# Attention fused with its graph prologue: ScalarE's and VectorE's instructions in the order of writing

## The chip, the cores and the metric

The kernel runs on one core of a Trainium2 chip. The metric is the device time of one execution in microseconds (us), as the median of several; it is compared between the kernel before and the kernel after the change.

## The reference

Inputs are x of 16 x 1024 x 256 (batch, nodes, channels) and adj of 1024 x 1024, all float32. Two layers are computed, each `x = layernorm(x + layer(x))`. The change concerns the first:

```python
fea = transpose(x, (0, 2, 1))                       # b, c, n
c_adj = mean(fea, axis=1)
diff = c_adj[:, None, :] - c_adj[:, :, None]
A = abs(abs(sigmoid(diff) - 0.5) - 0.5) * 2.0
Wg = adj * (A + transpose(A, (0, 2, 1))) * 0.5
g = relu(einsum('bcn,bnm->bcm', fea, Wg) * para)
q = g, transposed and split in 4 heads of 64
k, v = (x @ kv_w), split in 4 heads of 64
out = softmax(q @ k.T * scale) @ v
x = layernorm(x + out)
```

The second layer aggregates x with a normalised adj, and applies a linear layer, a batch normalisation, a relu, another linear layer and another batch normalisation. The changed lines do not touch it.

## The kernel before, in words

The work of the first layer goes batch element by batch element; what belongs to one of the 16 is called a block here. A block has two parts. The *prologue* (L642 to L748) makes q, k and v. The *attention* (L751 on) uses them. The prologue of block b + 1 is spread over the attention of block b, so that TensorE (PE) always has matmuls to do.

The prologue of a block has three lists. `first` holds four transposes of x through PE (`transpose_x`, L666, each into a PSUM tile of 512 columns that VectorE copies out, L674). The first of them also calls `begin` (L652): VectorE sums x over the channels (`csum`, L657) and makes `ccol` and `ncol`, SyncE's queue writes `ncol` to DRAM (L662) and reads it back spread over all partitions as `crow` (L664). `steps` holds 24 pieces for PE: four `values` (L720) and four `keys` (L708) in turn, and then 16 `graph_mm` (L689), of which four make one quarter of q: PE sums eight products of x with the weights `wg`, VectorE scales the sum (L703) and ScalarE applies relu (L706). `side` holds the pieces that make the eight weight tiles `wg` of 128 x 1024: ScalarE's abs (`weights_abs`, L679), ScalarE's tanh (L684) and, in the same piece as the tanh, VectorE's product with adj (L685).

The attention of a block has 2 pairs of heads times 2 halves of the queries times 8 key chunks, 32 units. A unit is: `scores` (L760), where PE writes 128 x 1024 scores into PSUM and ScalarE makes the exp (L773) into a tile `p`; and `outputs` (L776), where PE multiplies `p` with v (L789) and VectorE adds `p` to the running row sums `acc` (L796 and L798). After the eighth chunk ScalarE and VectorE take the sums of the outputs out of PSUM as `oT` (L802, L803). Two bursts later `normalise` (L805) sums `acc` over the partitions on PE, ScalarE and VectorE add the halves (`drow`, L818, L819), and SyncE's queue turns the row into a column by way of DRAM (L821, L824). Later still `residual` (L829) takes the reciprocal, transposes `oT` on PE (`poT`, L835), multiplies (`o`, L839), and GpSimd (POOL) adds the product to x (L844). After the last unit of a block the same function runs `layernorm` (L580 to L592) on the whole tile: eight statistics with their aggregates on VectorE, two small operations on POOL (L577, L579), eight scalings on VectorE (L590), and a store of x1 from POOL's queue (L847).

Two units make a *burst*; a block has 16, numbered u = 0 to 15. In each burst PE does the scores of this burst and then the outputs of the burst before, and then what the plan places there. `FULL` names the bursts that take four `steps`: 0, 4, 6, 8, 10, 12. Bursts 0 and 4 hold values and keys, the other four a quarter of q each. `residual` goes into bursts 8, 12, 0 and 4, `normalise` into 5, 9, 13 and 1. The two transposes of burst 10 and the two of burst 12 belong to the x of block b + 2, whose load is issued in burst 5. Before the first block a starting stretch makes the prologue of block 0 and the transposes of block 1.

What sets the order of the instructions: inside `tc.manual_schedule` (L862) PE issues in the order of writing. The other engines' order is made by the Tile scheduler, which may move an instruction ahead of others on its engine. The tiles come from pools: the scores have two PSUM tiles (`ps_s`), everything else in the prologue and in `normalise` and `residual` shares two PSUM tiles (`ps_t`, function `tile_t`), the outputs have two; `p` has four tiles, `wg` eight, `crow` one, x three.

Of the kernel before, what the change touches and what calls it, by code (L numbers as in the profile page):

```python
# [515 lines left out]
def fast_path(  # L516
# [19 lines left out]
    nc = tc.nc  # L536
# [3 lines left out]
    NCH = N // P  # L540
# [15 lines left out]
    def tile_t(name):  # L556
        return ps_t.tile([P, HALF], F32, tag="t", name=name)
# [4 lines left out]
    x1_d = [dram.tile([P, NCH, C], F32, tag=f"x1_{b}", name=f"x1_{b}") for b in range(B)]  # L562
# [11 lines left out]
    def rsqrt(dst, src, eps):  # L574
        n = dst.shape[1]
        if eps:
            nc.gpsimd.tensor_scalar(dst, src, eps, None, ALU.add)  # L577
            src = dst
        nc.gpsimd.tensor_tensor(dst, src, mhalf[:, :n], ALU.pow)  # L579

    def layernorm(t, name):
        st = small.tile([P, NCH, 6], F32, tag="ln_st", name=f"st_{name}")
        mv = small.tile([P, NCH, 2], F32, tag="ln_mv", name=f"mv_{name}")
        rstd = small.tile([P, NCH], F32, tag="ln_rs", name=f"rs_{name}")
        for n in range(NCH):
            nc.vector.bn_stats(st[:, n, :], t[:, n, :])
            nc.vector.bn_aggr(mv[:, n, :], st[:, n, :])
        rsqrt(rstd, mv[:, :, 1], EPS)
        for n in range(NCH):
            nc.vector.tensor_scalar(  # L590
                t[:, n, :], t[:, n, :], mv[:, n, 0:1], rstd[:, n : n + 1], ALU.subtract, ALU.mult
            )  # L592
# [20 lines left out]
    with (  # L613
# [15 lines left out]
        st = {}  # L629

        def load_x(b):
            t = xp.tile([P, NCH, C], F32, tag="x", name=f"x_{b}")
            nc.sync.dma_start(t, x[b].rearrange("(n p) c -> p n c", p=P))
            st[b] = {"x": t}
# [7 lines left out]
        def prologue(b):  # L642


            s = st[b]
            xt = s["x"]
            first, steps, side = [], [], []
# [34 lines left out]
            def weights_tanh(n):  # L682
                w = s["wg", n]
                nc.scalar.activation(w, w, AF.Tanh, scale=0.5)  # L684
                nc.vector.scalar_tensor_tensor(  # L685
                    w, w, 1.0, adj_s[:, n, :], op0=ALU.subtract, op1=ALU.mult
                )
# [57 lines left out]
            for n in range(NCH):  # L745
                side.append((weights_abs, (n,)))
                side.append((weights_tanh, (n,)))
            return first, steps, side  # L748


        PAIRS = H // 2  # L751
# [8 lines left out]
        def scores(i):  # L760
            b, pr, qh, m = units[i]
            qT, kT = st[b]["qT"], st[b]["kT"]
            ps = tile_s(f"ps_{i}")
            for kh in range(2):
                for hd in range(2):
                    r = slice(hd * D, (hd + 1) * D)
                    ks = slice(m * P + kh * D, m * P + (kh + 1) * D)
                    nc.tensor.matmul(  # L768
                        ps[kh * D : (kh + 1) * D, hd * HALF : (hd + 1) * HALF], kT[r, pr, ks],
                        qT[r, pr, qh * HALF : (qh + 1) * HALF], start=True, stop=True,  # L770
                    )
            p = pp.tile([P, N], F32, tag="p", name=f"p_{i}")
            nc.scalar.activation(p, ps, AF.Exp)  # L773
            A[i] = p

        def outputs(i):  # L776
            b, pr, qh, m = units[i]
            s, p = st[b], A.pop(i)
            if m == 0:
                G[b, pr, qh] = {  # L780
                    "po": [tile_o(f"po_{i}_{kh}") for kh in range(2)],
                    "acc": accp.tile([P, N], F32, tag="acc", name=f"acc_{i}"),
                }
            g = G[b, pr, qh]
            for hd in range(2):
                h = 2 * pr + hd
                for kh in range(2):
                    r = slice(kh * D, (kh + 1) * D)
                    nc.tensor.matmul(  # L789
                        g["po"][kh][hd * D : (hd + 1) * D, :], s["v"][r, m, h * D : (h + 1) * D],  # L790
                        p[r, hd * HALF : (hd + 1) * HALF], start=(m == 0), stop=(m == NCH - 1),
                    )
            if m == 0:
                g["p0"] = p
            elif m == 1:
                nc.vector.tensor_add(g["acc"], g.pop("p0"), p)  # L796
            else:
                nc.vector.tensor_add(g["acc"], g["acc"], p)  # L798
            if m == NCH - 1:
                k = (b * PAIRS + pr) * 2 + qh  # L800
                g["oT"] = op.tile([P, HALF], F32, tag="oT", name=f"oT_{k}")
                nc.scalar.copy(g["oT"], g["po"][0])  # L802
                nc.vector.tensor_add(g["oT"], g["po"][1], g["oT"])  # L803
# [25 lines left out]
        def residual(b, pr, qh):  # L829
            g, s = G.pop((b, pr, qh)), st[b]  # L830
            k = (b * PAIRS + pr) * 2 + qh
            nc.vector.reciprocal(r_all[:, k], g["col"])
            pt = tile_t(f"poT_{k}")
            for j in range(4):
                nc.tensor.transpose(  # L835
                    pt[:, j * P : (j + 1) * P], g["oT"][:, j * P : (j + 1) * P], ident
                )
            o = rdp.tile([P, 4, 2, D], F32, tag="o", name=f"o_{k}")
            nc.vector.tensor_mul(  # L839
                o, pt.rearrange("p (n h d) -> p n h d", h=2, d=D),  # L840
                r_all[:, k].unsqueeze(3).to_broadcast([P, 4, 2, D]),
            )
            xs = s["x"][:, 4 * qh : 4 * qh + 4, pr * P : (pr + 1) * P]
            nc.gpsimd.tensor_tensor(xs, xs, o.rearrange("p n h d -> p n (h d)"), ALU.add)  # L844
            if pr == PAIRS - 1 and qh == 1:
                layernorm(s["x"], f"l0_{b}")
                nc.gpsimd.dma_start(x1_d[b], s["x"])  # L847
                del st[b]

        def run(fs, k):  # L850
            for f, a in fs[:k]:
                f(*a)
            del fs[:k]
# [1 line left out]

        FULL = {0: 4, 4: 4, 6: 4, 8: 4, 10: 4, 12: 4}
        BURST = 2
        bursts = [range(i, i + BURST) for i in range(0, len(units), BURST)]  # L860
        PERB = PER // BURST
        with tc.manual_schedule(engines={mybir.EngineType.PE}):  # L862
            load_x(1)
            first, steps, side = prologue(0)
            run(first, 4)
            while steps:
                run(side, 4)
                run(steps, 2)
            next_first, next_steps, next_side = prologue(1)
            run(next_first, 4)  # L870
            run(next_side, 6)
            full, quarter = {}, {}

            def back(j):

                for i in bursts[j]:
                    outputs(i)
                b, pr, qh, m = units[bursts[j][-1]]
                if m == NCH - 1:
                    quarter.setdefault(j + 2, []).append((normalise, (b, pr, qh)))  # L880
                    k = j + 5
                    while k % PERB not in FULL:
                        k += 1
                    full.setdefault(k, []).append((residual, (b, pr, qh)))

            for j in range(len(bursts)):
                b, u = j // PERB, j % PERB
                for i in bursts[j]:
                    scores(i)
                run(quarter.get(j, []), 9)  # L890
                if u == 0:
                    steps, side = next_steps, next_side
                    next_first, next_steps, next_side = [], [], []
                if u == 5 and b + 2 < B:
                    load_x(b + 2)
                    next_first, next_steps, next_side = prologue(b + 2)
                if j:
                    back(j - 1)
                if u in FULL:
                    run(full.get(j, []), 9)  # L900
                    run(steps, FULL[u])
                    if u >= 10:
                        run(next_first, 2)
                if u > 12:
                    run(next_side, 2)
                else:
                    run(side, 1 if u in FULL else 2)
            j = len(bursts)
            back(j - 1)
            for k in range(j, j + 8):  # L910
                run(quarter.get(k, []), 9)
                run(full.get(k, []), 9)

        top = l0c.tile([P, 2], F32, name="top")
        nc.vector.tensor_reduce(top[:, 0:1], r_all, AX.XYZ, ALU.max)
# [275 lines left out]
```

## Time and profile before

| what | value |
|---|---|
| median of three runs | 2997.59 us (2993.03 to 2997.8) |
| profiled execution, its own time | 2992.18 us |
| profiled execution, its span | 2990.3 us |
| granted PE clock, mean | 0.947 |
| first scores (L768) start | 81.24 us |
| attention's last exp starts | 1862.38 us |
| one block (1004.36 to 1119.36) | 115.0 us |
| PE busy in that block | about 108.8 us of 115 |

The profile is one execution, recorded by the hardware. Times are counted from the span's start. A line of a timeline gives the start, the length, the engine, the source line, the operation with output and inputs, how many were merged, and in brackets how long the engine stood idle before it and what ended that wait. One burst of scores or outputs is 16 matmul instructions on PE. A busy time of PE is modelled at its end, so distances from start to start are used where it matters.

The attention stretch lasts from about 81 to 1866 us, the second layer fills the rest.

### The profile page before, as it was taken

How to read it: one execution, taken by the hardware profiler on the slowest of the kernel's cores; microseconds unless marked ns; L12 is line 12 of the kernel's file. 1: busy time of each engine (PE TensorE's matmuls, PEld its weight loads, DVE VectorE, ACT ScalarE, POOL GpSimd, SP SyncE). 2: the span in 40 equal slices, each digit the busy share in tenths (PEclk: the TensorE clock that was granted, in tenths of full speed). 3: DMA queues.
4: the chain of work that ended last, by engine and by line, in shares of the span. 5: the costliest groups of instructions: out<-in, count | busy, mean ns of one | idle time of the engine just before them, and what ended most of it. 6: DMA issues, size and time to landing. Idle time of an engine off the chain costs nothing. (4 is left out here: it accounts for less than half of the span.)

```text
span 2990.3 us, 32734 instructions
## 1 busy us (share of the span) xinstructions
PE 2736.4 (92%) x13522; PEld 1202.2 (40%) x13522; DVE 1418.0 (47%) x2130; ACT 1138.6 (38%) x1313; POOL 185.7 (6%) x196
## 2 busy tenths in 40 slices
PE   6999999999999999999999999799999999999842
PEld 3433334333333333334333333544444444344432
DVE  3565555655655665655655647511111212233464
ACT  3555354553553553553544535001101111233383
POOL 0000000000000000000000001000000000000032
PEclk9999999999999999999999999699999999999955
DMA  4001101101101001011011010022121220244265
GB/s 134 8 1 36 36 1 36 30 8 36 29 8 37 29 8 37 10 28 36 1 36 36 1 49 24 29 84 112 57 84 71 84 84 32 123 159 150 84 211 198
DMA packets 122062, 169.00 MB, mean 57 GB/s; under 512 B 86704, under 2 KB 103600, under 8 KB 111664
## 3 DMA queue, kind: packets, MB, share of 16 engines
q1 hardware_dynamic: 112720, 99.70, 10.9%
q0 software_dynamic: 9184, 67.12, 5.7%
q8 instruction: 108, 1.77, 0.3%
q14 instruction: 50, 0.41, 0.0%
HBM read 99.36 MB, written 67.44 MB: 56 GB/s over the span
## 5 line engine op out<-in xcount | busy, mean ns | idle before, releaser
L773 ACT ACTIVATE p<-ps 128x1024 f32<-128x1024 f32 x512 | 498.7, 1018 | 275.5 <-PE ps L768 263.6
L768 PE MATMUL ps<-qT,kT 64*64 64x512 f32 x4096 | 519.1, 619 | 69.6 <-ACT p L773 69.6
L798 DVE TENSOR_TENSOR acc<-acc,p 128x1024 f32<-128x1024 f32 x384 | 470.7, 1226 | 187.9 <-ACT p L773 174.8
L789 PE MATMUL po<-p,v 64*64 64x512 f32 x4096 | 500.4, 599 | 0.0
L697 PE MATMUL pg<-wg,x 128*128 128x512 f32 x1024 | 454.4, 597 | 4.3 <-ACT kT L718 4.3
L1003 PE MATMUL pagg<-ahT,x1l 128*128 128x512 f32 x1024 | 444.0, 593 | 0.0
L1022 ACT ACTIVATE hw<-ph,col_b 128x1024 f32<-128x1024 f32 x64 | 71.2, 1113 | 652.7 <-PE ph L1018 652.7
L768 PEld LDWEIGHTS ps<-qT,kT 64*64 64x64 f32 x4096 | 150.9, 137 | 368.1 <-issue 234.2
L1003 PEld LDWEIGHTS pagg<-ahT,x1l 128*128 128x128 f32 x1024 | 194.3, 190 | 241.1 <-issue 241.1
L697 PEld LDWEIGHTS pg<-wg,x 128*128 128x128 f32 x1024 | 190.2, 190 | 246.3 <-issue 216.6
L789 PEld LDWEIGHTS po<-p,v 64*64 64x64 f32 x4096 | 166.3, 137 | 292.8 <-issue 289.6
L1082 PE MATMUL po<-hl,w2T 128*128 128x512 f32 x512 | 222.8, 598 | 6.9 <-ACT hl L1073 6.9
L1018 PE MATMUL ph<-agg,w1T 128*128 128x512 f32 x512 | 222.2, 592 | 0.0
L1007 DVE COPY agg<-pagg 128x1024 f32<-128x1024 f32 x32 | 39.1, 1223 | 377.9 <-PE pagg L1003 377.9
L706 ACT ACTIVATE qT<-qT 128x512 f32<-128x512 f32 x64 | 40.1, 626 | 407.3 <-DVE qT L703 407.3
L685 DVE SCALAR_TENSOR_TENSOR wg<-wg,adj_s 128x1024 f32<-128x1024 f32 x128 | 153.3, 1220 | 77.0 <-ACT wg L684 77.0
L844 POOL TENSOR_TENSOR x<-x,o 128x512 f32<-128x512 f32 x64 | 81.1, 1267 | 1670.3 <-DVE o L839 1670.3
L1024 DVE BATCH_NORM_STATS2 bn_st<-hw 128x6 f32<-128x512 f32 x128 | 82.3, 685 | 152.4 <-ACT hw L1022 152.4
L727 PE MATMUL pv<-kvw_s,xT 128*128 128x256 f32 x512 | 128.0, 394 | 26.8 <-DVE v L731 16.1
L1082 PEld LDWEIGHTS po<-hl,w2T 128*128 128x128 f32 x512 | 98.3, 192 | 131.4 <-issue 121.9
L679 ACT ACTIVATE wg<-crow,ccol 128x1024 f32<-128x1024 f32 x128 | 140.8, 1137 | 17.2 <-PE pg L697 11.9
L1018 PEld LDWEIGHTS ph<-agg,w1T 128*128 128x128 f32 x512 | 97.3, 190 | 122.5 <-issue 122.5
(87 smaller groups left out, 1962.8 us busy)
## 6 DMA issues: line engine op xcount, KB each, us to landing
h<-hw POOLq DMA_DIRECT2D x16, 2048.0 KB, 6.6
hl<-h SPq DMA_DIRECT2D x16, 2048.0 KB
x<-in_x_dram SPq DMA_DIRECT2D x16, 1024.0 KB
x<-x POOLq DMA_DIRECT2D x16, 1024.0 KB, 4.3
x1l<-x SPq DMA_DIRECT2D x16, 1024.0 KB
xf<-x SPq DMA_DIRECT2D x16, 1024.0 KB
out_dram<-xf POOLq DMA_DIRECT2D x16, 1024.0 KB, 5.4
crow<-c SPq DMA_DIRECT2D x16, 512.0 KB
```

The source lines that it names most:

```text
L679: nc.scalar.activation(w, s["crow"], AF.Abs, bias=s["ccol"][:, n : n + 1])
L685: nc.vector.scalar_tensor_tensor(w, w, 1.0, adj_s[:, n, :], op0=ALU.subtract, op1=ALU.mult)
L697: nc.tensor.matmul(ps, xt[:, n, c * P : (c + 1) * P], s["wg", n][:, hs], start=(n == 0), stop=(n == NCH - 1),)
L727: nc.tensor.matmul(pt[:, j * C : (j + 1) * C], s["xT"][:, c, n * P : (n + 1) * P], kvw_s[:, c, C : 2 * C], start=(c == 0), stop=(c == CC - 1),
L768: nc.tensor.matmul(ps[kh * D : (kh + 1) * D, hd * HALF : (hd + 1) * HALF], kT[r, pr, ks], qT[r, pr, qh * HALF : (qh + 1) * HALF], start=Tr ...
L773: nc.scalar.activation(p, ps, AF.Exp)
L789: nc.tensor.matmul(g["po"][kh][hd * D : (hd + 1) * D, :], s["v"][r, m, h * D : (h + 1) * D], p[r, hd * HALF : (hd + 1) * HALF], start=(m = ...
L798: nc.vector.tensor_add(g["acc"], g["acc"], p)
L1003: nc.tensor.matmul(ps[:, hs], xt[:, m, c * P : (c + 1) * P], ahT[:, m, hs], start=(m == 0), stop=(m == NCH - 1),)
L1018: nc.tensor.matmul(ps[:, hs], w1T[:, c, k * P : (k + 1) * P], t[:, c, hs], start=(c == 0), stop=(c == CC - 1),)
L1024: nc.vector.bn_stats(bn1_st[:, k, 2 * b + half, :], ht[:, k, half * HALF : (half + 1) * HALF])
L1082: nc.tensor.matmul(ps[:, hs], w2T[:, k, c * P : (c + 1) * P], ht[:, k, hs], start=(k == 0), stop=(k == HC - 1),)
```

## The change

ScalarE and VectorE are added to the engines that issue in the order of writing. To suit that, the pieces of the prologue are placed anew: the product with adj becomes a piece of its own (`weights_adj`), one weight behind the tanh; a table `SIDE` says how many side pieces follow each burst, and bursts 0 and 4 take two side pieces after each of their four steps; one of the two transposes in bursts 10 and 12 moves ahead of the graph matmuls; the layernorm of a block becomes a function of its own (`finish_x1`), which is run in the burst after the last residual (burst 5), ahead of the x load and prologue of block b + 2. At the start, six side pieces instead of four go with two steps, and four side pieces of block 1 instead of six stand ahead of block 0. The set of computing instructions is the same, and each is of the same size.

```diff
@@ prologue
             def weights_tanh(n):
                 w = s["wg", n]
                 nc.scalar.activation(w, w, AF.Tanh, scale=0.5)
+
+            def weights_adj(n):
+                w = s["wg", n]
                 nc.vector.scalar_tensor_tensor(
                     w, w, 1.0, adj_s[:, n, :], op0=ALU.subtract, op1=ALU.mult
                 )
...
             for n in range(NCH):
                 side.append((weights_abs, (n,)))
                 side.append((weights_tanh, (n,)))
+                if n:
+                    side.append((weights_adj, (n - 1,)))
+            side.append((weights_adj, (NCH - 1,)))
@@ residual
-            if pr == PAIRS - 1 and qh == 1:
-                layernorm(s["x"], f"l0_{b}")
-                nc.gpsimd.dma_start(x1_d[b], s["x"])
-                del st[b]
+
+        def finish_x1(b):
+            xt = st.pop(b)["x"]
+            layernorm(xt, f"l0_{b}")
+            nc.gpsimd.dma_start(x1_d[b], xt)
@@ the plan
-        FULL = {0: 4, 4: 4, 6: 4, 8: 4, 10: 4, 12: 4}
...
-        with tc.manual_schedule(engines={mybir.EngineType.PE}):
+        FULL = (0, 4, 6, 8, 10, 12)
+        SIDE = {13: 1, 14: 1, 15: 1, 1: 1, 2: 1, 3: 1, 5: 4}
+        with tc.manual_schedule(engines={mybir.EngineType.PE, mybir.EngineType.Activation, mybir.EngineType.DVE}):
             load_x(1)
             first, steps, side = prologue(0)
             run(first, 4)
             while steps:
-                run(side, 4)
+                run(side, 6)
                 run(steps, 2)
             next_first, next_steps, next_side = prologue(1)
             run(next_first, 4)
-            run(next_side, 6)
-            full, quarter = {}, {}
+            run(next_side, 4)
+            full, quarter, late = {}, {}, {}
...
                     full.setdefault(k, []).append((residual, (b, pr, qh)))
+                    if pr == PAIRS - 1 and qh == 1:
+                        late.setdefault(k + 1, []).append((finish_x1, (b,)))
...
                     next_first, next_steps, next_side = [], [], []
+                if j:
+                    back(j - 1)
+                run(late.get(j, []), 9)
                 if u == 5 and b + 2 < B:
                     load_x(b + 2)
                     next_first, next_steps, next_side = prologue(b + 2)
-                if j:
-                    back(j - 1)
                 if u in FULL:
                     run(full.get(j, []), 9)
-                    run(steps, FULL[u])
                     if u >= 10:
-                        run(next_first, 2)
-                if u > 12:
-                    run(next_side, 2)
+                        run(next_first, 1)
+                    for _ in range(4):
+                        run(steps, 1)
+                        if u <= 4:
+                            run(side, 2)
+                    if u >= 10:
+                        run(next_first, 1)
+                elif u > 12:
+                    run(next_side, SIDE[u])
                 else:
-                    run(side, 1 if u in FULL else 2)
+                    run(side, SIDE.get(u, 0))
```

More of the change, by code (lines that the diff above doesn't have):

```diff
@@ L912, in fast_path @@
                 run(full.get(k, []), 9)
+                run(late.get(k, []), 9)
         top = l0c.tile([P, 2], F32, name="top")
```

## The prediction

> **What bounds the kernel now.** I read the busy shares and slices first, then PE's waits between 100 and 1850 us, then one block (one batch element's attention, 16 bursts) as a timeline, engine by engine, then the start. TensorE is 92% busy, VectorE 47%, ScalarE 38%: only time in which PE stands still, or runs slowly, can be won.
>
> ```profile
> PE 2736.4 (92%) x13522; PEld 1202.2 (40%) x13522; DVE 1418.0 (47%) x2130; ACT 1138.6 (38%) x1313; POOL 185.7 (6%) x196
> ```
>
> PE's waits in the attention stretch (engine, line, awaited: us, times, longest): the scores wait for the exp that frees their PSUM tile. Values wait for a copy, transposes for the q eviction.
>
> ```profile
> PE ps L768 <- ACT p L773: 69.6, 20, 4.5
> PE pv L727 <- DVE v L731: 12.7, 14, 0.9
> PE pxT L671 <- DVE qT L703: 9.7, 28, 0.3
> ```
>
> One such wait on PE's timeline, at the end of a block: 4.45 us idle, then a burst of 3.69 us and one of 2.59 instead of 1.9.
>
> ```profile
> 1103.57 1.92 PE L789 MATMUL po<-p,v 64*64 64x512 f32 x16
> 1109.94 3.69 PE L768 MATMUL ps<-qT,kT 64*64 64x512 f32 x16 [4.45 <-ACT p L773]
> 1113.41 2.59 PE L789 MATMUL po<-p,v 64*64 64x512 f32 x16
> 1115.83 1.89 PE L768 MATMUL ps<-qT,kT 64*64 64x512 f32 x16
> ```
>
> ScalarE at that moment: weight pieces stand ahead of the two exps, whose scores were written by 1103.7.
>
> ```profile
> 1103.95 1.06 ACT L684 ACTIVATE wg<-wg 128x1024 f32<-128x1024 f32 x1
> 1104.91 2.18 ACT L679 ACTIVATE wg<-crow,ccol 128x1024 f32<-128x1024 f32 x2
> 1106.99 1.99 ACT L684 ACTIVATE wg<-wg 128x1024 f32<-128x1024 f32 x2
> 1108.88 1.91 ACT L773 ACTIVATE p<-ps 128x1024 f32<-128x1024 f32 x2
> ```
>
> VectorE's layernorm holds a round trip through POOL; the start has ScalarE waiting for crow, then the first exp at 83.41:
>
> ```profile
> 1034.15 2.67 DVE L590 TENSOR_SCALAR x<-x,mv_l,rs_l 128x256 f32<-128x256 f32 x8 [2.12 <-POOL rs_l L579]
> 36.46 2.19 ACT L679 ACTIVATE wg<-crow,ccol 128x1024 f32<-128x1024 f32 x2 [5.29 <-DMA crow<-c]
> 83.41 1.00 ACT L773 ACTIVATE p<-ps 128x1024 f32<-128x1024 f32 x1
> ```
>
> **What the Trainium skill says.** "TensorE: Matmul & The Clock Gate", Part 1: an idle window of about 3.4 us halves PE's clock, and busy time restores it. The trace agrees: all 14 waits of 4.45 us are followed by a burst of 3.00 to 3.69 us; the one of 2.07 us by 2.46, one of 1.42 by 2.00. The same page, Architectural detail: ScalarE and VectorE queues are strict FIFO; the exps above show it. "ScalarE: Activation LUTs", Table sets: exp, tanh and abs share one set, so interleaving them loads no tables; the trace has one load (1.28 us) in all. "VectorE: DVE Perf Modes", The DRAIN you can't avoid: a semaphore on the engine's own last result costs nothing beyond the drain. The trace differs a little: two accumulations that depend on each other stand 1.31 us apart, two independent weight products 1.14.
>
> **The change, part by part.** Both orders were read from the built programs. Durations are of the profiled execution.
>
> *Removed.* (1) Weight pieces now stand singly between bursts (abs in 13, tanh in 14, abs in 15), the rest under the wide bursts 0 and 4. A plain burst has 3.43 us of PE against 1.94 for two exps, so a piece of 1.04 to 1.14 fits. The 14 waits go: each is 4.65 (idle between planned and real start) plus 1.75 and 0.70 of slow clock, 7.1 us: 99.4. (2) Layernorm leaves bursts 0 and 4: 15 value waits of 0.91: 13.7. (3) One transpose moves ahead of the graph matmuls: 28 x 0.35: 9.8. (4) The mean of the next x moves from VectorE's place right behind the load to burst 10: four waits of exps, 5.0. Together 128.
>
> *Added at burst 6, blocks 1 to 14.* VectorE's order in burst 5 is: denominator row, one accumulation, whole layernorm, weight products 6 and 7. From the start of burst 5: ScalarE has the last k copy to 0.7 (0.58), abs to 1.7, tanh to 2.8 (it waits for abs), two exps to 4.65, row copy to 5.15. VectorE, behind that copy: row add 0.68 and accumulation 1.22, to 7.0; eight statistics, each 0.39 plus an aggregate of 0.17 that waits for it, 4.0 to 4.5, to 11.3; POOL 2.12, to 13.4; eight scalings 2.67, to 16.05; product 6 at 17.2, 7 at 18.4. PE: burst 5 is 1.77 + 0.86 + 1.72 = 4.35, burst 6's scores and outputs 3.54, six of eight graph products 5.23: it needs weight 6 at 13.1. Gap 4.1 us, and with it the slow clock of a 4.45 gap, 2.45: 6.55 x 14 = 91.7. Queued behind on VectorE are the accumulations that free p for the exps of burst 7; at slow clock PE comes there later than they do (0), at full clock 0.5 us late.
>
> *Added at burst 12.* The new transpose stands between poT and the graph, and both PSUM tiles are then taken. The graph waits for o, which now stands behind the oT add, behind ScalarE's oT copy: copy ends 4.25 us after the burst's start, add 5.0, reciprocal 5.1, o 5.85; PE was ready at 4.6: 1.3 x 14 = 18.2. In bursts 0 and 4 k waits likewise, 0.13 x 29 = 3.8.
>
> *Added at the start.* VectorE and ScalarE can't run ahead any more. Table load behind crow's wait: abs starts at 37.8 not 36.46. Values copies and k copies stand among the weight pieces; eight pairs of 2.15 and two k copies of 0.6 end at 56.5, the last k copy at 57.1, graph from there instead of 49.0: ends 86.0 instead of 78.3. Only then does VectorE take block 1's x mean (2.29 + 0.25, it ran at 34.51 and before), then the write of c (SP's wait for it: median 8.1, 8.5 in the block read) and crow (4.06 from issue to use at the start): abs of block 1 at 101.9. Two abs/tanh pairs of 2.15 stand ahead of the first exp: 106.2 instead of 83.41. PE stands still for a k tile meanwhile; burst 2 starts at 116.5 instead of 95.2: 21. Bounds: c 8.1 to 10.9, crow 2 to 4.1, PE cold or not: 18 to 26.
>
> *Last block, 3.4.* In burst 5 layernorm has no wide burst over it: the row copy comes earlier (exps from 1.1 to 3.05, copy 3.65), row add and accumulation end at 5.5, statistics at 9.8, POOL 11.95, scalings 14.6, and the exps of burst 7 wait for accumulation 5 at 15.8, where they could start at 8.9; PE loses 6.2, 8.6 with its clock, where the block loses 5.2 now. *After attention, 6.5.* Four of the eight row sums of adj ran beside PE's column sums; in the new order all eight stand behind the weight copies that need PE: 4 x 1.34, and the check of the denominators, which PE's column sums stand behind, comes 1 later. SP's and POOL's order of DMAs stays: the x load waits for the x1 store, which ends some 18 us ahead of its use at burst 10, and that is free.
>
> Sum: -128 + 91.7 + 18.2 + 3.8 + 21 + 3.4 + 6.5 = +16.6 us. Made against the profiled execution (span 2990.3, time 2992.2) it gives 3008.8; the median shown is 2997.6, 5.4 above it, so I forecast 3014.
>
> What is unseen is a layernorm as one block on VectorE (4.0 to 4.5 for its statistics; POOL 1.65 to 2.12), and a gap of 3 to 4 us: its clock loss lies between 0.5 (the 2.07 gap) and 2.45. Burst 6 thus costs 3.5 to 7.2, 49 to 101 in all; I take 6.55, since every gap near it paid in full.
>
> **Rivals.** *A, faster:* the chain in burst 5 ends earlier, or PE's idle time stays under what trips the clock. Decides at a gap of about 3 us: then 3 + 1.2 = 4.2 x 14 = 59, and the sum is -16: 2981; at 2 us, -41: 2957. For it: statistics that overlap as they do now, the next starting before an aggregate ends. Against: every link has its row. *B, all stalls go:* layernorm hides, PE is fed throughout: -75, 2922. Against: PE's queue reaches weight 6 at 13.1, and layernorm alone is 9. *C, slower still:* late accumulations hold the exps of bursts 6 to 8 too, or the statistics take over 5 us: 1 to 1.8 more a block, or the start 5 more: 3035. *D, nothing changes:* needs an unchanged order; 14 blocks have another.
>
> **How the numbers follow.** A measurement can tell about 0.2% (6 us) from no change. Forecast 0.55, its own range 2997 to 3030; A 0.26, B 0.04, C 0.14, D 0.01. Faster: A mostly and B: 0.28. Same: the lower edge of the forecast and A's upper: 0.12. Slower 0.60. The range cuts B, a little of A and of C: 2964 to 3042.
>
> **What would show it.** The exp's 4.45 waits gone; a wait of graph matmuls (L700 in the changed file) for the weight products (L688 there) of about 4 us, 14 times, with a slow burst behind; waits of graph for o (L845 there), 1.3 us, 14 times; the first exp near 106; the attention's end later by some 10 us; adj's scaling later still by 6. Wrong if the L700 wait is under 3 us or the clock holds, or the first exp comes before 100.

## The result, and the profile after

| | before | after |
|---|---|---|
| median, us | 2995.59 (2993.03 to 2997.8) | 2995.57 (2991.16 to 2996.58) |
| profiled execution, its own time | 2992.18 | 2996.41 |
| its span, and granted PE clock | 2990.3, 0.947 | 2994.5, 0.944 |

The ratio of after to before is 0.9997 (95% interval 0.998 to 1.0015): no difference that can be measured. The forecast was 3014 us, slower.

PE is 91% busy, VectorE 48%, ScalarE 38%, nearly as before. PE's waits between 100 and 1850 us in the profile after, all of them (engine, line, awaited; us in total, times, longest):

```profile
PE pg L700 <- DVE wg L688: 54.7, 14, 3.9
PE pg L700 <- DVE o L845: 18.5, 14, 1.3
PE pk L717 <- DVE v L734: 11.4, 1, 11.4
PE ps L774 <- ACT p L779: 5.3, 1, 5.3
```

So the 20 waits for exps (one is left, in the last block), the value waits and the transpose waits are gone. In their place stand the graph's waits for a weight product and for `o`, and one wait at the start. Bursts 14 and 15, which held a stall of 4.45, now take 3.43 us each in every block.

Here is a burst 6 on PE's timeline; its burst 5 began at 925.92.

```profile
933.80 5.42 PE L700 MATMUL pg<-wg,x 128*128 128x512 f32 x12
943.13 3.21 PE L700 MATMUL pg<-wg,x 128*128 128x512 f32 x4 [3.91 <-DVE wg L688]
946.27 2.56 PE L774 MATMUL ps<-qT,kT 64*64 64x512 f32 x16
948.66 1.89 PE L795 MATMUL po<-p,v 64*64 64x512 f32 x16
```

Twelve instructions run, then PE waits 3.91 us; the next four take 3.21 instead of 1.88, and the scores 2.56 instead of 1.95. VectorE holds it up, with accumulation, layernorm and products one after the other (most of the statistics are left out at the dots):

```profile
931.69 1.22 DVE L802 TENSOR_TENSOR acc<-p,p 128x1024 f32<-128x1024 f32 x1
932.82 0.42 DVE L586 BATCH_NORM_STATS2 st_l<-x 128x6 f32<-128x256 f32 x1
...
939.27 2.67 DVE L590 TENSOR_SCALAR x<-x,mv_l,rs_l 128x256 f32<-128x256 f32 x8 [2.12 <-POOL rs_l L579]
941.86 2.35 DVE L688 SCALAR_TENSOR_TENSOR wg<-wg,adj_s 128x1024 f32<-128x1024 f32 x2
```

The start: ScalarE waits 17.36 us for the crow of block 1, and the exps of burst 0 come at 110.23 instead of 83.41, behind two pairs of abs and tanh.

```profile
105.96 1.15 ACT L679 ACTIVATE wg<-crow,ccol 128x1024 f32<-128x1024 f32 x1 [17.36 <-DMA crow<-c]
110.23 1.92 ACT L779 ACTIVATE p<-ps 128x1024 f32<-128x1024 f32 x2
```

Burst 12, then adj's first transposes behind the attention (their wait was 8.29):

```profile
986.59 3.70 PE L700 MATMUL pg<-wg,x 128*128 128x512 f32 x8 [1.32 <-DVE o L845]
1924.54 1.05 PE L1004 MATMUL pah<-ident,adj_s 128*128 128x128 f32 x2 [14.10 <-DVE adj_s L999]
```

Distances between the starts of successive bursts of scores on PE give a ledger of the whole difference between the two spans. "Predicted" is the sum on record; "measured" is after minus before in the two profiled executions, in us. Terms that share a stretch are put together (the prediction's 6.5 behind the attention as 1 and 5.5).

| stretch | predicted | measured |
|---|---|---|
| start, to burst 2 of block 0 (95.21, then 120.50) | +21 | +25.3 |
| stalls at a block's end with their clock (bursts 14, 15) | -99.4 | -96.3 |
| value and k waits (bursts 0, 4, 5) | -9.9 | -15.2 |
| burst 6 with its clock (bursts 6, 7) | +91.7 | +85.8 |
| exps behind the mean of x (bursts 7, 8) | -5.0 | -8.2 |
| transposes and `o` (bursts 10, 12) | +8.4 | +5.7 |
| last block, to the check of the denominators | +4.4 | +0.6 |
| behind it, to the end | +5.5 | +6.5 |
| sum | +16.6 | +4.2 |

### The profile page after: what moved, and what is told of

It reads as the page before. It is cut to its first block, busy times and chain, and to the rows that moved or that the text cites. A ratio compares the mean times of both kernels' runs of the same rounds, so it can differ in the third digit from the quotient of the medians.

```text
span 2994.5 us, 32707 instructions
## 1 busy us (share of the span) xinstructions
PE 2728.1 (91%) x13522; PEld 1207.1 (40%) x13522; DVE 1447.7 (48%) x2130; ACT 1143.0 (38%) x1313; POOL 185.5 (6%) x196
## 5 line engine op out<-in xcount | busy, mean ns | idle before, releaser
L700 PE MATMUL pg<-wg,x 128*128 128x512 f32 x1024 | 477.8, 619 | 74.8 <-DVE wg L688 54.7
L774 PE MATMUL ps<-qT,kT 64*64 64x512 f32 x4096 | 500.5, 604 | 5.3 <-ACT p L779 5.3
L795 PE MATMUL po<-p,v 64*64 64x512 f32 x4096 | 486.7, 589 | 0.0
L688 DVE SCALAR_TENSOR_TENSOR wg<-wg,adj_s 128x1024 f32<-128x1024 f32 x128 | 168.6, 1336 | 49.3 <-ACT wg L684 49.3
L706 DVE SCALAR_TENSOR_TENSOR qT<-pg,para_s 128x512 f32<-128x512 f32 x64 | 44.2, 691 | 274.0 <-PE pg L700 273.9
L679 ACT ACTIVATE wg<-crow,ccol 128x1024 f32<-128x1024 f32 x128 | 147.5, 1152 | 17.4 <-DMA crow<-c 17.4
```

Of the source, the lines that this page charges most:

```text
L679: nc.scalar.activation(w, s["crow"], AF.Abs, bias=s["ccol"][:, n : n + 1])
L688: nc.vector.scalar_tensor_tensor(w, w, 1.0, adj_s[:, n, :], op0=ALU.subtract, op1=ALU.mult)
L700: nc.tensor.matmul(ps, xt[:, n, c * P : (c + 1) * P], s["wg", n][:, hs], start=(n == 0), stop=(n == NCH - 1),)
L774: nc.tensor.matmul(ps[kh * D : (kh + 1) * D, hd * HALF : (hd + 1) * HALF], kT[r, pr, ks], qT[r, pr, qh * HALF : (qh + 1) * HALF], start=Tr ...
L795: nc.tensor.matmul(g["po"][kh][hd * D : (hd + 1) * D, :], s["v"][r, m, h * D : (h + 1) * D], p[r, hd * HALF : (hd + 1) * HALF], start=(m = ...
```

## The experiments

Each is the changed kernel with one edit, unless said otherwise. Ratios are to the kernel before on the same chip (medians of it there 2995.4 to 2997.0), with their 95% intervals.

**1. The whole layernorm one burst later.**

```diff
-                        late.setdefault(k + 1, []).append((finish_x1, (b,)))
+                        late.setdefault(k + 2, []).append((finish_x1, (b,)))
-                if u == 5 and b + 2 < B:
+                if u == 6 and b + 2 < B:
```

> The changed kernel with the layernorm of a block, the store of x1 and the load of x for block b + 2 one burst later (burst 6, under that burst's own graph matmuls, instead of burst 5 ahead of weight products 6 and 7). Theory 1 (the change won its 128 us and paid them back mostly in burst 6): the 14 waits of the graph matmuls for the weight product (3.9 us each, 54.7 in all) and the slow clock behind them (2.2 each, 31 in all) both go, burst 6 and 7 take 10.6 and 3.5 us again, and the time is 86 under the changed kernel's 2995.6: 2910, within 2902 to 2918. Theory 2 (the time in burst 6 is only borrowed: a layernorm of 9 us on VectorE is late somewhere in any burst): the scaling of q and the accumulations come behind it, the exps of burst 8 wait for a tile p, and 1.5 to 3 us a block come back: 2931 to 2952. Theory 3 (the slow clock in burst 6 does not come from the gap): only the 55 go: 2941, with slow bursts still there without a gap.

Measured 2998.45, ratio 1.0003 (0.9994 to 1.0012): nothing won, which not even theory 2 had expected. The wait for the product is gone and another has its size (the sum of PE's new waits, then PE and ScalarE in one block):

```profile
PE ps L774 <- ACT p L779: 64.2, 15, 4.4
```

```profile
948.97 3.69 PE L774 MATMUL ps<-qT,kT 64*64 64x512 f32 x16 [4.30 <-ACT p L779]
```

```profile
947.37 0.63 ACT L709 ACTIVATE qT<-qT 128x512 f32<-128x512 f32 x1 [12.30 <-DVE qT L706]
947.91 1.92 ACT L779 ACTIVATE p<-ps 128x1024 f32<-128x1024 f32 x2
```

ScalarE stands idle for 12.30 us, more than 4 of them with the scores of burst 7 written (PE began them at 941.00): relu is next in its written order, and relu waits for VectorE's scaling of q behind the layernorm.

**2. That relu alone, on top of experiment 1**, put behind the exps of burst 7.

```diff
-                    nc.scalar.activation(q, q, AF.Relu)
+                    if b > 1 and c == 0 and half == 0:
+                        relu.append((nc.scalar.activation, (q, q, AF.Relu)))
+                    else:
+                        nc.scalar.activation(q, q, AF.Relu)
...
+                if u == 7:
+                    run(relu, 1)
```

> As the run with the whole layernorm in burst 6, but ScalarE's relu of the first quarter of q stands behind the exps of burst 7 instead of ahead of them. Nothing else moves, VectorE's order is the same. Theory 1 (the gap of 4.3 us in that run was the relu's place in ScalarE's fixed order, not VectorE's length): the exps of burst 7 start 1.8 us after their scores, those of burst 8 wait for accumulations only to 4 us after that burst's start, which its graph matmuls cover; no gap: 2910, within 2903 to 2918, as with the layernorm in two parts. Theory 2 (VectorE is the limit): the exps of burst 7 or 8 wait for accumulations, 2945 to 2996.

Measured 2907.81, ratio 0.9707 (0.9692 to 0.9722): theory 1. VectorE's order is that of experiment 1; one ScalarE instruction of 0.63 us in another place is worth some 90 us. The exps no longer wait for it (they start at 903.23, the relu is behind them):

```profile
903.23 1.94 ACT L783 ACTIVATE p<-ps 128x1024 f32<-128x1024 f32 x2 [7.14 <-PE ps L778]
908.40 0.63 ACT L863 ACTIVATE qT<-qT 128x512 f32<-128x512 f32 x1 [3.23 <-DVE qT L706]
```

**3. The products ahead of the layernorm within burst 5.**

```diff
+                if u == 5:
+                    run(side, 4)
                 run(late.get(j, []), 9)
```

> The changed kernel with the four side pieces of burst 5 (the last abs and tanh, weight products 6 and 7) ahead of the layernorm in the order of writing. The products are there 4 us before PE asks for them, but the layernorm then ends 18.4 us from the start of burst 5, the accumulations of burst 5 at 20.9, the scaling of q at 21.6, ScalarE's relu at 22.2, and the exps of burst 7 stand behind it, which PE needs at 18.4. Theory 1 (what counts is the last of the fixed chain from VectorE over relu to the exps): the gap moves from the weight product to the exp and grows to 4.8 us: 3008, within 2998 to 3018. Theory 2 (the gap is the order of layernorm and products alone): gone, 2910 to 2920.

Measured 3001.54, ratio 1.0020 (1.0009 to 1.0030): theory 1. The wait for the product is gone, and PE waits for exps, 65.6 us in 15 waits against 64.2 in experiment 1, at the same place.

**4. The layernorm in two parts**: statistics and POOL's step (`ln_stats`, a function of its own now, not shown) in burst 6, scalings and store in burst 7.

```diff
-                        late.setdefault(k + 1, []).append((finish_x1, (b,)))
+                        late.setdefault(k + 2, []).append((ln_stats, (b,)))
+                        late.setdefault(k + 3, []).append((finish_x1, (b,)))
-                if u == 5 and b + 2 < B:
+                if u == 7 and b + 2 < B:
```

> The changed kernel with the layernorm of a block cut in two: statistics and the reciprocal root in burst 6, between the accumulations of that burst and the scaling of q; scalings and store of x1 in burst 7 behind its accumulations; the load of x for block b + 2 behind that, in burst 7. In the run with the whole layernorm in burst 6 the 14 gaps only moved: the scaling of q stood behind it, ScalarE's relu behind that, and the exps of burst 7 behind the relu (4.3 us each). Theory 1 (VectorE has room for 9 us of layernorm in bursts 6 and 7, only not in one piece): accumulations to 3.5 us from the start of burst 6, statistics to 7.7, POOL to 9.8, scaling of q at 10.7 when PE is done, accumulations to 13.9, scalings to 16.6; nothing of PE waits, both the gaps and the slow clock go: 86 less, 2910, within 2903 to 2918, blocks 1 to 14 at 107.2 us. Theory 2 (9 us of VectorE are missing in every block wherever they are put): a wait of 2 to 4 us moves on, to the exps of burst 8 or to the transposes of burst 10 behind the later load of x: 2945 to 2996.

Measured 2906.7, ratio 0.9709 (0.9694 to 0.9723): theory 1. Bursts 6 and 7 take 10.61 and 3.48 in every block, and a block 107.0 on average instead of 113.1. VectorE had the time for the whole layernorm; it had none for it in one piece at that place.

**5. More work for PE in the gap**, eight matmuls and then four, whose sum nothing reads.

```diff
+                if b > 1 and c == 0 and half == 0 and part == 3:
+                    pd = tile_t(f"pd_{b}")
+                    for n in range(8):
+                        nc.tensor.matmul(
+                            pd, xt[:, n, 0:P], s["wg", 0][:, hs], start=True, stop=True
+                        )
```

> The changed kernel with eight more matmuls of 512 columns in burst 6 of blocks 1 to 14, between the sixth and the seventh product of the first graph quarter; their sum goes to a PSUM tile that nothing reads. They add work only: 8 x 0.43 = 3.4 us of PE at full clock, in the place where PE now stands still for 3.9 us. Theory 1 (31 of the 86 us that burst 6 costs are PE's slow clock, which comes of standing still): the wait shrinks to about 0.5, the clock stays up, bursts 6 and 7 together take 18.3 to 18.8 us instead of 20.2, and the kernel gets 20 to 27 us faster by doing more: 2971, within 2964 to 2980. Theory 2 (the slow clock comes of something else in that burst, such as the layernorm's traffic): no change or slower, 2994 to 3010.

Measured 3002.03, ratio 1.0019 (1.0011 to 1.0027). The time lies in the range of theory 2, but the trace shows another reason. The added work had twice the size that was meant: a matmul of 512 columns is two instructions here, and the eight take 6.87 us, not 3.4. As theory 1 had it, no wait for the product is left and the scores of burst 7 follow at full speed; bursts 6 and 7 take 17.47 and 3.48, only 0.73 more than the 20.22 of the changed kernel, for 6.87 us of added work. With four (`range(4)`):

> As the run with eight added matmuls in burst 6, but with four: one of 512 columns takes 0.86 us (two instructions of 0.43), so that four are the 3.4 us that were meant; the eight took 6.87 and left no gap. Theory 1 (31 of the 86 us are slow clock that comes of standing still): wait for the weight product 0.5 us, the clock stays up, bursts 6 and 7 take 18.0 to 18.6 us instead of 20.2: 22 to 31 us faster by doing more, 2969, within 2963 to 2976. Theory 2 (the added work only fills the gap, the slow clock comes of something else): 2994 to 3000.

Measured 2972.24, ratio 0.9924 (0.9911 to 0.9938): theory 1. Useless work made the kernel some 23 us faster; bursts 6 and 7 take 18.6. PE's line in the gap, and the next scores:

```profile
926.70 3.60 PE L702 MATMUL pd<-wg,x 128*128 128x512 f32 x8
930.76 2.26 PE L706 MATMUL pg<-wg,x 128*128 128x512 f32 x4 [0.47 <-DVE wg L688]
932.95 1.95 PE L780 MATMUL ps<-qT,kT 64*64 64x512 f32 x16
```

What is above 1.88 in the second line (0.38) is the wait for product 7 inside the group, and the scores take 1.95 at once, not 2.56: the slow clock comes of PE standing still.

**6. Half of the statistics in burst 2**, to make the gap smaller; the rest of the layernorm stays in burst 5 (`ln_stats` here takes one half; not shown).

```diff
+                        late.setdefault(k - 2, []).append((ln_stats, (b, 0)))
                         late.setdefault(k + 1, []).append((finish_x1, (b,)))
```

> The changed kernel with the layernorm's statistics of the first four rows of tiles, which are complete after the residual of burst 0, moved to burst 2; the other half, POOL's step and the scalings stay in burst 5. The gap in burst 6 shrinks from 3.9 by half the statistics (2.1) to 1.8 us. Theory 1 (the clock loss has a threshold between 2 and 4 us): bursts 6 and 7 lose 1.8 and at most 0.5 more, 2.3 instead of 6.1 a block: 2995.6 - 53 = 2942, within 2937 to 2946. Theory 2 (the clock loss is in proportion to the gap): 1.8 + 1.0: 2949, within 2946 to 2953. Theory 3 (VectorE has no room in burst 2 either): the exps of burst 4 wait for accumulations there, and 1 us a block comes back: 2955 or more.

Measured 2957.17, ratio 0.9872 (0.9857 to 0.9887). Burst 6 behaved: the gap is 1.81, and bursts 6 and 7 lose 2.37 us in most blocks (gap, 0.38 for product 7, the rest small) and 4.0 in three of the 14, where the clock went down. What missed is near theory 3: not exps, but the keys of burst 4 wait, for `o`, which VectorE now reaches later: 14 times, 16.1 us in all, and the burst takes 12.44 instead of 11.32.

**7. The starting stretch in another order.** The mean of x (`mean`) is split off `begin` for this (not shown).

```diff
-            while steps:
-                run(side, 6)
-                run(steps, 2)
-            next_first, next_steps, next_side = prologue(1)
-            run(next_first, 4)
-            run(next_side, 4)
+            run(steps, 8)
+            run(side, 24)
+            next_first, next_steps, next_side = prologue(1)
+            st[1]["mean"]()
+            run(steps, 13)
+            run(next_side, 4)
+            run(steps, 3)
+            run(next_first, 4)
```

> The changed kernel with another order in the starting stretch alone: values and keys of block 0 ahead of its weight pieces, the mean of block 1's x (and with it the write of c and the read of crow) behind the weight pieces instead of behind the graph matmuls, the first weight pieces of block 1 in the last quarter of the graph. Theory 1 (the start costs 25.3 us in the profiled pair, because ScalarE and VectorE cannot run ahead of the written order): first exp near 84 instead of 110.2, burst 2 of block 0 near 96 instead of 120.5, the rest unchanged: 2995.6 - 25 = 2971, within 2966 to 2977. Theory 2 (the start is bound by the DMA round trip of c and crow whatever the order): first exp stays after 100, and no more than 8 us go (the earlier graph): 2987 to 2996.

Measured 2969.23, ratio 0.9902 (0.9886 to 0.9919): theory 1. First exp at 83.32, burst 2 at 94.61. The written order cost 26 us here, and another written order costs nothing.

**8. Burst 12's two transposes behind the graph.**

```diff
-                    if u >= 10:
+                    if u == 10:
                         run(next_first, 1)
...
                     if u >= 10:
-                        run(next_first, 1)
+                        run(next_first, u // 6)
```

> The changed kernel with both transposes of x in burst 12 behind the graph matmuls, as before the change; burst 10 keeps one ahead and one behind. Theory 1 (the transpose between poT and the graph takes the second PSUM tile, so that the graph waits for o): the 14 waits of 1.3 us of the graph matmuls for o go, the second transpose waits 0.35 us again, burst 12 takes 12.44 instead of 13.46: 14 x 1.02 = 14.3 less: 2981, within 2977 to 2986. Theory 2 (o is late whatever stands there, because it stands behind the sum oT on VectorE): the graph then waits for it in another place and the time stays at 2995.

Measured 2984.5, ratio 0.9957 (0.9941 to 0.9972): theory 1, 11 us; the waits for `o` are gone and burst 12 takes 12.34 instead of 13.29 on average.

**9. Edits 1, 7 and 8 together.**

> The changed kernel with all three edits: layernorm in burst 6, the starting stretch reordered, both transposes of burst 12 behind the graph. Theory 1 (the three are separate costs, and add up): 2995.6 - 86 - 25 - 14 = 2870, within 2862 to 2880, with blocks 1 to 14 at 106 to 107 us each. Theory 2 (they hide one another): 2890 or more.

Measured 2959.96, ratio 0.9869 (0.9848 to 0.9890). 7 and 8 add up (26 + 11 from 2996 is 2959); edit 1, of which the text expected 86, brings nothing here as it brought nothing alone.

**10. Placement without order, order without placement, and ScalarE's order alone.** Only the engines of `tc.manual_schedule` are edited; the second starts from the kernel before, the others from the changed one.

```diff
-tc.manual_schedule(engines={mybir.EngineType.PE, mybir.EngineType.Activation, mybir.EngineType.DVE}):
+tc.manual_schedule(engines={mybir.EngineType.PE}):
```

> The changed kernel's placement of the pieces, but only PE issues in the order of writing; ScalarE's and VectorE's order is the scheduler's again. In that order seven weight pieces stand in a row ahead of the exps of burst 0, and the layernorm is spread over the value copies of bursts 0 and 4. Theory 1 (the order of writing brings both the gain and the loss, the placement alone brings neither): the exps' waits at a block's end are back, about 7 us each, no gap in burst 6, the start as before the change: the kernel before again, 2996, within 2980 to 3015. Theory 2 (the placement alone brings the gain and the written order the loss): 2992 - 100 = 2892 to 2920.

Measured 3000.0, ratio 1.0016 (1.0009 to 1.0023): theory 1, if anything a little slower. PE's waits for exps come to 86.0 us here, against 69.6 before the change.

> The kernel before with its placement of the pieces, but ScalarE and VectorE issue in the order of writing. The weight pieces stand two by two between the bursts, so that the exps' waits at a block's end shrink from 7 us to 1 or less; but the layernorm stands whole in burst 4 ahead of the last value copies, and the values behind them wait. Theory 1 (in a written order a layernorm of 9 us costs its length less the cover of the burst it stands in): values in burst 4 wait about 6 us and pay 2.4 of slow clock, 15 x 8.4 = 126, start and end 31 more, exps 99 - 15 less: 2992 + 126 + 31 - 84 - 14 = 3051, within 3025 to 3085. Theory 2 (the written order itself is the gain, wherever the pieces stand): 2920 to 2960.

Measured 3064.72, ratio 1.0237 (1.0221 to 1.0253): theory 1. Bursts 14 and 15 take 3.43 each as in the changed kernel, so that the order alone takes the stalls away, even with two pieces a burst; but burst 4 takes 20.1 instead of 12.2, PE waiting for value copies behind the layernorm:

```profile
964.43 3.59 PE L714 MATMUL pk<-xT,kvw_s 128*128 128x512 f32 x4 [4.98 <-DVE v L731]
```

With PE and Activation as the engines:

> The changed kernel, but of the two engines only ScalarE issues in the order of writing (with PE, as before); VectorE's order is the scheduler's again, which spreads the layernorm over the value copies of bursts 0 and 4 and takes the mean of the next x early. Theory 1 (the gain comes of ScalarE's order, the loss of VectorE's): no wait of exps at a block's end, no gap in burst 6, the value waits of 0.9 a block back, the start some 10 us shorter than in the changed kernel: 2995.6 - 86 + 14 - 10 = 2914, within 2895 to 2935. Theory 2 (with pieces that ScalarE takes in a fixed order, VectorE's own order delays the products and the accumulations): 2950 to 3000, with waits for products or exps in bursts 0 to 5.

Measured 2945.78, ratio 0.9844 (0.9825 to 0.9862): between the two. The stalls at a block's end and the gap in burst 6 are both gone, so with this placement ScalarE's order is enough to win what the change won at a block's end. But the scheduler puts the mean of the next x early in VectorE's order, and VectorE then waits for the load of x with accumulations and q's scaling behind it; ScalarE's fixed order passes that on over relu to the exps:

```profile
911.87 2.29 DVE L657 TENSOR_REDUCE csum<-x 128x8 f32<-128x2048 f32 x1 [6.69 <-DMA x<-in_x_dram]
```

```profile
918.91 3.69 PE L774 MATMUL ps<-qT,kT 64*64 64x512 f32 x16 [4.29 <-ACT p L779]
```

**11. The repairs together**: edits 4, 7 and 8.

> The layernorm in two parts, the reordered starting stretch and both transposes of burst 12 behind the graph, together, on the changed kernel. Theory 1 (separate costs add up): 2995.6 - 86 - 26 - 11 = 2872, within 2864 to 2880, blocks 1 to 14 at 106.3 us each. Theory 2 (VectorE lacks the time wherever the layernorm is put): 2910 to 2960.

Measured 2867.2, ratio 0.9578 (0.9565 to 0.9591): theory 1; it beats both kernels by 128 us, the size of what the prediction counted as removed. A block takes 106.03 us on average. Between 95 and 1730 us PE's waits, whole:

```profile
PE pxT L674 <- DVE qT L709: 4.9, 14, 0.3
PE den L823 <- DVE acc L808: 4.0, 1, 4.0
```

With one more transpose moved, and behind the attention `transpose_weights` behind the row sums of adj in the text:

```diff
-                        run(next_first, u // 6)
+                        run(next_first, 1)
...
+                    if u == 11:
+                        run(next_first, 1)
```

> The kernel with the layernorm in two parts, the reordered start and the transposes of burst 12 behind the graph (2867.2), with two more moves: the first transpose of burst 12 into burst 11, so that none waits 0.35 us for the scaling of q, and behind the attention the row sums of adj ahead of the weight copies. Theory 1: 14 x 0.35 = 5 and the 5.8 us of the longer wait ahead of adj's transposes go: 2867 - 11 = 2856, within 2850 to 2862. Theory 2 (the end of the attention is bound by PE's column sums and the DMAs anyway): 2860 to 2867.

Measured 2864.57, ratio 0.9561 (0.9548 to 0.9574), an interval that overlaps that of the run before: theory 2. Bursts 11 and 12 take 15.58 instead of 15.82, and adj's transposes still wait 13.7 us. What would shorten that wait stays open.

## Why the prediction was wrong, point by point

**Bounds and removals: right in kind.** The stalls that it named are gone, for 96.3 us against 99.4; experiment 10 shows that the order of writing does it, not the placement. The term for the mean of x was too small (5.0, measured 8.2): it counted four waits and left out the slow clock behind the longest of them. That wait, in the profile before:

```profile
362.47 2.46 PE L768 MATMUL ps<-qT,kT 64*64 64x512 f32 x16 [2.07 <-ACT p L773]
364.69 3.20 PE L789 MATMUL po<-p,v 64*64 64x512 f32 x16
```

The prediction read 0.5 us of slow clock from the first line. The second is slow too, 3.20 instead of 1.90, so that it is 1.8 us in all; the prediction's lower bound for the clock loss of a gap of 3 to 4 us, taken from this one, was too low.

**The burst-5 chain: right, link by link.** In the trace, from the start of burst 5, the accumulation ends at 7.0, the statistics at 11.2, POOL at 13.35, the scalings at 16.0 and product 6 at 17.2; no link is off by more than 0.1. PE asked at 13.3, not 13.1, so the gap is 3.91, not 4.1. Experiment 5 shows that the gap causes the clock loss.

**Burst 12 and the start: right in kind.** The wait for `o` is 1.32 us, 14 times, as written. The first exp was put at 106.2 and came at 110.23; experiments 7 and 8 take both terms away and the time falls by them.

**The step that failed is the sum, by the sizes of its terms, and what was made of it**: "-128 + 91.7 + 18.2 + 3.8 + 21 + 3.4 + 6.5 = +16.6 us". The profiled pair measured +4.2. These terms were mis-sized:

- Burst 6, "6.55 x 14 = 91.7": measured 85.8. It took 2.45 us of slow clock for every gap from the one block that it had read. There the slow clock lasted 6.83 us; in the profile after it lasted 3.41 us in eleven of the 14 blocks, and clock and product 7 together cost 2.2 on average. In the profile before, five of the 14 stalls had the short slow clock too, so the stalls gave 3.1 less than was counted.
- Bursts 0, 4 and 5 gained 5.3 more: the waits of k, "0.13 x 29 = 3.8", are not in the trace, and the bursts gave 15.2 where 13.7 was counted for the value waits.
- The last block with the check behind it cost 0.6 instead of 4.4: its wait for exps was 5.31, not 6.2, and the stretch from the last scores to the check got 1.6 shorter instead of 1 longer. Why it did stays open.
- The mean of x gave 3.2 more, and bursts 10 and 12 cost 2.7 less.
- The other way, the start cost 4.3 more and the end 1.0 more.

None of these is over 6 us, but together they are 12.4. As +16.6 is what is left of -128 and +145, an error of a few per cent in each is as large as the result.

The second part of the miss is the carry: "the median shown is 2997.6, 5.4 above it, so I forecast 3014". That offset belonged to one execution. Before's profiled execution lies 3.4 below the median of before's four runs, after's lies 0.8 above its own. So 3014 misses by 18.4: 12.4 from the sum, 6.2 from the carry, less rounding. The prediction also had no rival in which the two large sums cancel, and gave "same" only 0.12.

**The rivals.** A wanted a gap under 3 or a clock that holds; neither came. B, PE fed throughout, did not come either; it is what the edits of experiments 2 and 4 made of the kernel: 2907, where B had 2922. Of C only the start's 4 us came. D was an unchanged order; the time was unchanged with every large wait in another place.

## What to carry to other kernels

When two engines go over to the written order, go through every instruction that can wait and ask what stands behind it in that engine's queue, and then what stands behind that one's reader: with one relu of 0.63 us ahead of the exps, moving the layernorm only moved a 4 us gap; with the relu behind them the same kernel was 90 us faster. When a forecast is the rest of two large sums, give its sign no more trust than their errors allow, and look for the gain by undoing the added waits one by one: all 128 us were there. A long side job such as a layernorm can be cut where its engine waits for another one (experiment 4); moving what stands behind it did as much here (experiment 2).

## What the runs showed of the hardware that was not expected

PE's slow clock is a cost that can be bought off with work: about 3.4 us of matmuls in a gap of 3.9 won some 23 us in 14 blocks.

The Trainium skill, "TensorE: Matmul & The Clock Gate", Part 1, puts an idle window of about 3.4 us ahead of the slower clock and calls the window free-running. The traces agree on the window, but it need not be idle throughout: already the gap of 2.07 us in the kernel before was followed by the slow clock. Every change of the granted clock that the 17 profiles record lies, within its profile, on a grid of 3.41 us, to 0.01 us. Here are three steps of that grid around the gap of 3.91 us in burst 6 (start and end; length; busy time and instructions of PE, its weight loads, VectorE, ScalarE and POOL; granted clock; DMA's share and GB/s):

```profile
937.33:940.74 3.41, 1.89 (x5) 0.57 (x3) 1.47 (x5) 0.00 (x0) 1.82 (x2) 1.00 0.00 0
940.74:944.15 3.41, 1.02 (x2) 0.30 (x2) 3.41 (x7) 0.00 (x0) 0.62 (x1) 1.00 0.25 106
944.15:947.57 3.42, 3.41 (x11) 1.05 (x14) 3.39 (x5) 0.33 (x1) 0.00 (x0) 0.50 0.49 201
```

PE stands still for 1.52 us of the first step and 2.39 us of the second, and only behind the second is the clock halved. The same count over all 17 profiles, from 130 to 1720 us, has 7706 steps at full clock. All 134 with 1.97 us of idle time or more were followed by a slow one, none with less than 1.7; in between it was three of 28. A slow step with less than 0.6 us of idle time was the last, one with more than 0.7 was followed by another. So the slow clock lasted 3.41 or 6.83 us: in the changed kernel eleven blocks had the first and lost 5.6 to 6.0 us in bursts 6 and 7, three had the second and lost 7.1 to 7.2, for the same gap of 3.91. Where a gap falls on the grid thus counts beside its length. The gaps of 1.81 us in experiment 6, three of 14 followed by the slow clock, are in the range where both occur. No run here shifts a gap against the grid and leaves all else alone, so this rests on the gaps as they fell.
